# A state-space layer with a routed expert layer: the state-space part in a new pinned order, with other layouts for U and Y

## The chip, the cores and the metric

The kernel runs on one core of a Trainium2 chip. The metric is device time in microseconds (us) of one execution. The engines are called as the profile calls them: PE (matrix products; PEld is its weight load), DVE (vector), ACT (scalar, activation functions), POOL (GpSimd), and SP, whose queue issues most DMAs.

## The reference

Input x has 2 sequences of 2048 tokens with 128 channels. What is computed, cut to its core:

```python
def attn(x):                                   # on layernorm(x), as B=2 sequences
    u = swapaxes(x @ in_W.T + in_b, 1, 2)      # (B, D, L)
    dtA = (-exp(log_A_real) + 1j * A_imag) * exp(log_dt)[:, None]
    K = exp(dtA[:, :, None] * arange(L))       # 128 channels x 32 modes x L
    k = 2 * einsum('hn,hnl->hl', C * (exp(dtA) - 1) / A, K).real
    y = irfft(rfft(u, 2 * L) * rfft(k, 2 * L))[..., :L] + u * D_skip[:, None]
    a, g = split(glu_W @ gelu(y) + glu_b, 2)
    return swapaxes(a * sigmoid(g), 1, 2) @ out_W.T + out_b + x
def ffn(x):
    gates = softmax(x @ router_w)              # 14 routed experts, top 2, renormalised
    return sum over the top 2 of gate * expert(x) + shared_0(x) + shared_1(x)
x = x + attn(layernorm(x));  x = x + ffn(layernorm(x))   # expert: silu(rmsnorm(x) @ W1) @ W2
```

## The kernel before

**Tiles.** The 4096 tokens are 32 chunks of 128 (`NT` = 32, 16 per sequence). The long convolution is done chunk by chunk: inside a chunk by a 128 x 128 Toeplitz matrix per channel, between chunks by the 32 complex modes of each channel. Modes lie on partitions: 128 partitions are 4 channels x 32 modes, and `q` (`NQ` = 32) counts the groups of 4 channels, in four groups of 8 called group 0 to 3.

**State-space part, lines 173 to 537.** Token means (L189), turned copies of X through PE into XT, which is the memory of Y (L197, L198), and squares (L200) are on ACT. The mode arithmetic on DVE (L146 to L276, with two Sin on ACT, L237 and L238) ends in Z, the powers 1, 2, 4 ... 128 of each mode's factor. `double` (L292 to L301) builds PW, all powers 0 to 127, by seven doublings of four DVE operations each; the first five go over all q, the last two (m = 32, 64) over one group at a time. For each group follow

- `taps`: products of PW with BC on PE (L314, L319), four ACT copies into kk (L327), and a DMA of kk to memory (L329),
- `toeplitz`: DMAs that read the Toeplitz matrices back, 1 MB for each of 8 channel groups `toep[g]` (L344); numbers 5 and 6 go into the memory of Y, 0 to 4 and 7 share five buffers,
- `turned`: transposes of PW on PE (L353) and ACT copies into VT (L354).

Then `scales` (L362 to L369: reciprocal square roots on DVE, a product with `flip` on PE that turns them round), and `project` (L375 on PE, L380 on DVE), which make U, laid out chunk by chunk: `U[:, c, :]` is a chunk's 128 channels. Channel `h` of all chunks is therefore `U[:, :, h]`, 32 elements 512 B apart. L401 normalises X on ACT. W and E (L404 to L422, DVE) are the modes' powers over whole chunks. `chunk_sums` (L441, PE) reads VT and `U[:, :, h]`; `scan` (L465 to L486, DVE, once for each half of q) makes the states ST; `inside` (L509, PE) multiplies `U[:, :, h]` by the Toeplitz matrices, and L527 adds the states' part to the same PSUM tiles ("corrections"). Four of the eight channel groups are one half. After each half four Gelu (L533, ACT) write YC, and one DVE transpose of 32 x 32 blocks writes Y (L537), through a view with the token outermost.

**Gating and routing, lines 623 to 830.** Eight blocks of four chunks pass through `products` (pg, pa from Y on PE), `gate` (tanh `th` and `av` on ACT), `gated` (DVE), `project` (po), `add`, `scales`, `rows`, `logits`, `choose`, `count` and `scatter`; the last writes each token's row twice by indirect DMAs from POOL (L817, 64 in all). The shared experts run in between. All of these operations carry line 623, a helper. Their order is written out at the end of the function.

**Experts and end.** The loop over 45 tiles of routed rows (L889, L899, L908), then the sums per token.

**What sets the order.** A planner orders each engine's instructions and places the waits, except for those that pass through `tc.keep_in_program_order`: these keep the order of the program text on their engine. Before, V, S and T are wrapped so (class `Ordered`, L616) only from the gating part on; in the state-space part the planner is free, and it mixes, for instance, W's first operations into `scales`. The experts' loop is free again.

Of the kernel before, what the change touches and what calls it, by code (L numbers as in the profile page):

```python
# [18 lines left out]
P = 128  # L19
# [35 lines left out]
def swapped(ap):  # L55

    dims = [list(d) for d in ap.ap]
    step = dims[1][0]
    return bass.AP(ap.tensor, ap.offset + step, [dims[0], [-step, 2]] + dims[2:])


@with_exitstack
def s4d_glu_moe_kernel(
# [108 lines left out]
    Y = tokp.tile([P, NT, P], F32, name="Y")  # L172

    with ExitStack() as ssm:
        big = ssm.enter_context(tc.tile_pool(name="big", bufs=1))
        rot = ssm.enter_context(tc.tile_pool(name="rot", bufs=2))
        pss = ssm.enter_context(tc.tile_pool(name="pss", bufs=4, space=PSUM))


# [6 lines left out]
        XT = Y  # L186
        for b in range(B):
            for k in range(b * NCH, (b + 1) * NCH):
                S.activation(junk, X[:, k, :], AF.Copy, accum_out=nm[:, k:k + 1])  # L189
            G.tensor_scalar(  # L190
                nm[:, b * NCH:(b + 1) * NCH], nm[:, b * NCH:(b + 1) * NCH], -1.0 / P, None,
                ALU.mult,
            )
        for g in range(NB):
            pt = pss.tile([P, TB, P], F32, name=f"pt_{g}", tag="ps")
            for k in range(TB):
                T.matmul(pt[:, k, :], lhsT=X[:, g * TB + k, :], rhs=flip, start=True, stop=True)  # L197
            S.copy(XT[:, g * TB:(g + 1) * TB, :], pt)  # L198
        for k in range(NT):
            S.activation(  # L200
                junk, X[:, k, :], AF.Square, bias=nm[:, k:k + 1], accum_out=sq[:, k:k + 1]
            )

        cent = big.tile([P, P], F32, name="cent")
        G.tensor_scalar(cent, ident, 1.0 / P, None, ALU.subtract)
        pc = pss.tile([P, P], F32, name="pc", tag="ps")
        T.matmul(pc, lhsT=cent, rhs=inw, start=True, stop=True)
        inwc = big.tile([P, P], F32, name="inwc")
        S.copy(inwc, pc)
# [34 lines left out]


        R7 = big.tile([P, NQ], F32, name="R7")
        CS = big.tile([P, 2, NQ], F32, name="CS")
        S.copy(R7, mag[:, 7 * NQ:])
        S.copy(CS[:, 0], s2[:, 7 * NQ:])
        S.copy(CS[:, 1], s1[:, 7 * NQ:])  # L250

# [27 lines left out]
        tpp = ssm.enter_context(tc.tile_pool(name="toep", bufs=5))  # L279
# [8 lines left out]
        for c, x in ((0, 0), (1, 2)):  # L288
            V.tensor_tensor(
                BC[:, c], bc(CE[:, x], 2, 8), mask.rearrange("p g i a r -> p (g i a) r"), ALU.mult  # L290
            )

# [14 lines left out]
        def taps(g):  # L307
# [16 lines left out]
            kk = rot.tile([P, 2 * P], F32, name=f"kk_{g}", tag="kk", bufs=4)  # L324
            G.memset(kk, 0.0)
# [6 lines left out]
        def toeplitz(g):  # L332

            if g in (5, 6):
                tg = Y[:, 16 * (g - 5):16 * (g - 4), :]
            else:
                tg = tpp.tile([P, 4 * GQ, P], F32, name=f"toep_{g}", tag="toep")
# [18 lines left out]
        U = big.tile([P, NT, P], F32, name="U")  # L356
        rsr = big.tile([P, NT], F32, name="rsr")

        def scales():

            tc.keep_in_program_order(
                V.tensor_scalar(sq, sq, 1.0 / P, LN_EPS, ALU.mult, ALU.add)  # L362
            )
# [3 lines left out]
            V.tensor_copy(rsr, pf)  # L367
            V.tensor_tensor(nb, nm, rs, ALU.mult)
            V.tensor_scalar(rs1, rs, 1.0, None, ALU.add)  # L369

        def project(g):
            pu = pss.tile([P, TB, P], F32, name=f"pu_{g}", tag="ps")
            for k in range(TB):
                c = g * TB + k
                T.matmul(  # L375
                    pu[:, k, :], lhsT=XT[:, c, :], rhs=inwc, start=True, stop=True
                )
            for k in range(TB):
                c = g * TB + k
                V.scalar_tensor_tensor(  # L380
                    U[:, c, :], pu[:, k, :], rsr[:, c:c + 1], inb, ALU.mult, ALU.add
                )

        for m in (1, 2, 4, 8, 16):
            double(slice(0, NQ), m)
        for g in range(4):
# [3 lines left out]
            for n in (2 * g, 2 * g + 1):  # L390
                if n < 5:
                    toeplitz(n)
            turned(g)
        scales()
        for b in range(NB):
            project(b)
        toeplitz(5)
        toeplitz(6)

        for k in range(NT):  # L400
# [3 lines left out]


        W = big.tile([P, 2, NQ, NCH], F32, name="W")
        E = big.tile([P, 2, NQ, NCH], F32, name="E")
        V.tensor_copy(W[:, :, :, 0], CS)
        for m in (1, 2, 4, 8):
            t1 = rot.tile([P, 2, NQ, m], F32, name="t1w", tag="t1", bufs=1)  # L410
            t2 = rot.tile([P, 2, NQ, m], F32, name="t2w", tag="t2", bufs=1)
            low, top = W[:, :, :, 0:m], W[:, :, :, m - 1]
            V.tensor_tensor(t1, low, bc(bc(top[:, 0], 1, 2), 3, m), ALU.mult)
            V.tensor_tensor(t2, low, bc(bc(top[:, 1], 1, 2), 3, m), ALU.mult)
            V.tensor_tensor(W[:, 0, :, m:2 * m], t1[:, 0], t2[:, 1], ALU.subtract)
            V.tensor_tensor(W[:, 1, :, m:2 * m], t1[:, 1], t2[:, 0], ALU.add)
        t1 = rot.tile([P, 2, NQ, NCH], F32, name="t1e", tag="t1", bufs=1)
        t2 = rot.tile([P, 2, NQ, NCH], F32, name="t2e", tag="t2", bufs=1)
        V.tensor_tensor(t1, bc(CE[:, 0:2], 3, NCH), bc(W[:, 0], 1, 2), ALU.mult)
        V.tensor_tensor(t2, bc(CE[:, 0:2], 3, NCH), bc(W[:, 1], 1, 2), ALU.mult)  # L420
        V.tensor_tensor(E[:, 0], t1[:, 0], t2[:, 1], ALU.add)
        V.tensor_tensor(E[:, 1], t1[:, 1], t2[:, 0], ALU.subtract)  # L422

        RA = big.tile([P, NQ * B, NCH], F32, name="RA")
        G.memset(RA[:, :, 0:1], 0.0)
        S.copy(
            RA[:, :, 1:].rearrange("p (q b) i -> p q b i", b=B), bc(bc(R7, 2, B), 3, NCH - 1)
        )
        ST = big.tile([P, 2, NQ, NT], F32, name="ST")
        G.memset(ST.rearrange("p c q (b i) -> p (c q b) i", b=B)[:, :, 0:1], 0.0)  # L430

        HQ = NQ // 2
        with tc.tile_pool(name="psS", bufs=2, space=PSUM) as psS:

            def chunk_sums(x):

                sp = psS.tile([P, 2, HQ, NT], F32, name=f"SP_{x}", tag="sp")
                for q in range(x * HQ, (x + 1) * HQ):
                    for c in range(2):
                        for j in range(4):  # L440
                            T.matmul(  # L441
                                sp[j * NM:(j + 1) * NM, c, q - x * HQ, :],
                                lhsT=VT[:, c, q, j * NM:(j + 1) * NM], rhs=U[:, :, 4 * q + j],
                                start=True, stop=True,
                            )
                return sp

            def scan(x, sp):


                qs = slice(x * HQ, (x + 1) * HQ)
                er, ei = bc(E[:, 0, qs], 2, B), bc(E[:, 1, qs], 2, B)
                wr, wi = (bc(W[:, c, qs, :NCH - 1], 2, B) for c in range(2))

                def four(what, n):
                    ts = [
                        rot.tile([P, 2, HQ, B, n], F32, name=f"{what}{i}_{x}", tag=f"t{i}", bufs=1)
                        for i in (1, 2)
                    ]
                    return [t[:, i] for t in ts for i in range(2)]  # L460

                s0, s1 = (sp[:, c].rearrange("p q (b i) -> p q b i", b=B) for c in range(2))
                D = rot.tile([P, 2, HQ, B, NCH], F32, name=f"D_{x}", tag="D", bufs=1)
                a, b, c, d = four("d", NCH)
                V.tensor_tensor(a, s0, er, ALU.mult)  # L465
                V.tensor_tensor(b, s1, ei, ALU.mult)
                V.tensor_tensor(D[:, 0], a, b, ALU.subtract)
                V.tensor_tensor(c, s0, ei, ALU.mult)
                V.tensor_tensor(d, s1, er, ALU.mult)
                V.tensor_tensor(D[:, 1], c, d, ALU.add)  # L470
                QS = rot.tile([P, 2, HQ, B, NCH], F32, name=f"QS_{x}", tag="QS", bufs=1)
                for i in range(2):
                    V.tensor_tensor_scan(
                        QS[:, i].rearrange("p q b i -> p (q b i)"),
                        RA[:, B * qs.start:B * qs.stop, :].rearrange("p q i -> p (q i)"),
                        D[:, i].rearrange("p q b i -> p (q b i)"), 0.0, ALU.mult, ALU.add,
                    )
                a, b, c, d = four("e", NCH - 1)
                q0, q1 = QS[:, 0, :, :, :NCH - 1], QS[:, 1, :, :, :NCH - 1]
                st = ST[:, :, qs].rearrange("p c q (b i) -> p c q b i", b=B)[:, :, :, :, 1:]  # L480
                V.tensor_tensor(a, q0, wr, ALU.mult)
# [670 lines left out]
```

## Time and profile before

| | |
|---|---|
| median of 3 runs | 402.42 us (401.95 to 404.42) |
| the profiled execution | 408.15 us |
| its span, first to last instruction | 406.1 us |
| mean granted PE clock | 0.848 |
| busy PE, DVE, ACT, POOL | 292.5, 223.2, 169.4, 161.3 us |
| transpose into Y ends | 123.1 us |
| first scatter, last scatter issued | 148.2, 252.0 us |

The profiled execution is 5.7 us longer than the median, so times read from its rows are set against its own span, and only differences are carried over to the median. A row of the timeline has the start, the duration, the engine, the line, the operation, its output and inputs, and their shapes; in square brackets stands how long the engine had been idle, and what ended that. A row of the groups has the busy time and the mean of one in ns, then the idle time before. Neighbouring rows of one engine can overlap a little, so the time that an instruction really takes on its engine is the distance from start to start.

### The profile page before, as it was taken

The page shows a single profiled execution, that of the slowest core. Times are in us where ns is not written, and L with a number is a line of the kernel's source. Part 1 is how long each engine was busy: PE and PEld are TensorE (multiplying, and loading weights), DVE is VectorE, ACT ScalarE, POOL GpSimd, SP SyncE. Part 2 cuts the span into 40 slices and gives each one's busy share as a digit, 9 for nine tenths or more (in the row PEclk, how much of TensorE's full clock was granted, in tenths as well). Part 3 has the DMA queues.
Part 4 walks back from the last instruction along what each step waited for, and adds up shares of the span by engine and source line. Part 5 has one row for each costly group of instructions (what it writes and reads, how often), then busy time and mean ns, then how long its engine had stood idle before and what let it go on. Part 6 is the DMA issues. An engine that isn't in the chain of part 4 may idle for free. (4 is left out here: it accounts for less than half of the span.)

```text
span 406.1 us, 7923 instructions
## 1 busy us (share of the span) xinstructions
PE 292.5 (72%) x2800; PEld 236.8 (58%) x2800; DVE 223.2 (55%) x654; ACT 169.4 (42%) x388; POOL 161.3 (40%) x243
## 2 busy tenths in 40 slices
PE   2702777788907647999999956599988879799500
PEld 2701567787903433768676644499977768797400
DVE  5699989899753662774958330133332333231074
ACT  3999869400431526485857502122222212132100
POOL 4300000000002034027677777057777777777500
PEclk9965889899965866696968989599999999899955
DMA  8100379913006911001111112665555555630098
GB/s 232 24 1 2 85 209 248 241 46 64 5 0 216 347 50 39 2 7 52 49 52 53 54 53 78 225 231 192 197 195 198 195 196 184 213 111 17 4 370 246
DMA packets 58089, 50.63 MB, mean 125 GB/s; under 512 B 6669, under 2 KB 50203, under 8 KB 58050
## 3 DMA queue, kind: packets, MB, share of 16 engines
q1 hardware_dynamic: 51010, 40.60, 32.8%
q0 software_dynamic: 4928, 8.48, 6.1%
q10 hardware_dynamic: 2112, 1.05, 0.9%
q8 instruction: 22, 0.36, 0.4%
q14 instruction: 17, 0.14, 0.1%
HBM read 25.36 MB, written 14.64 MB: 98 GB/s over the span
## 5 line engine op out<-in xcount | busy, mean ns | idle before, releaser
L908 POOL DMA_INDIRECT res<-yo,xg x90 | 88.6, 984 | 41.3 <-issue 19.8
L817 POOL DMA_INDIRECT xs_rows<-pl,si x64 | 62.0, 969 | 65.4 <-issue 39.1
L891 ACT ACTIVATE hs<-ph 128x512 f32<-128x512 f32 x45 | 26.9, 597 | 90.8 <-PE ph L889 90.8
L904 DVE TENSOR_TENSOR yo<-pz,xg 128x256 f32<-128x256 f32 x45 | 19.1, 424 | 60.9 <-PE pz L899 49.7
L899 PEld LDWEIGHTS pz<-wg,hs 128*128 128x128 f32 x360 | 48.0, 195 | 2.4
L889 PE MATMUL ph<-xgt,wg 128*128 128x256 f32 x180 | 49.4, 401 | 0.0
L899 PE MATMUL pz<-wg,hs 128*128 128x128 f32 x360 | 48.0, 278 | 0.0
L582 POOL MEMSET blank<- 128x260 f32 x1 | 0.3, 315 | 96.1 <-DVE Y L537 96.1
L889 PEld LDWEIGHTS ph<-xgt,wg 128*128 128x128 f32 x180 | 32.8, 203 | 3.0
L881 PE MATMUL xgt<-ident,xg 128*128 128x128 f32 x90 | 19.6, 302 | 18.3 <-DMA xg<-xs_rows 18.1
L883 DVE COPY xgt<-xgt 128x256 f32<-128x256 f32 x45 | 18.8, 418 | 22.4 <-PE xgt L881 22.3
L623 PE MATMUL ph<-XRT,WB 128*128 128x512 f32 x48 | 27.0, 712 | 0.3 <-ACT hsh L623 0.3
L623 ACT ACTIVATE hsh<-ph 128x512 f32<-128x512 f32 x24 | 14.1, 597 | 28.6 <-PE ph L623 28.6
L623 PEld LDWEIGHTS pz<-WB,hsh 128*128 128x128 f32 x192 | 22.9, 192 | 3.8 <-issue 3.6
L881 PEld LDWEIGHTS xgt<-ident,xg 128*128 128x128 f32 x90 | 10.9, 149 | 22.8 <-DMA xg<-xs_rows 21.4
L623 PE MATMUL pz<-WB,hsh 128*128 128x128 f32 x192 | 23.1, 275 | 0.0
L314 PE MATMUL kps<-PW,BC 128*8 128x128 f32 x128 | 5.6, 307 | 21.9 <-ACT junk L200 18.4
L623 PE MATMUL po<-outwh,y 128*128 128x128 f32 x64 | 15.4, 427 | 7.7 <-DVE y L623 7.7
L623 PEld LDWEIGHTS po<-outwh,y 128*128 128x128 f32 x64 | 14.0, 326 | 10.2 <-issue 6.8
L623 PE MATMUL pg<-Y,gluw 128*128 128x512 f32 x16 | 12.0, 844 | 10.8 <-DVE Y L537 10.8
L623 PEld LDWEIGHTS ph<-XRT,WB 128*128 128x128 f32 x48 | 10.7, 236 | 12.4 <-issue 10.7
L441 PE MATMUL SP<-U,VT 128*32 128x32 f32 x512 | 13.9, 301 | 5.5 <-issue 3.0
(236 smaller groups left out, 569.3 us busy)
## 6 DMA issues: line engine op xcount, KB each, us to landing
wg<-WB SPq DMA_DIRECT2D x45, 256.0 KB, 2.7
toep<-kp SPq DMA_DIRECT2D x24, 256.0 KB, 6.3
xg<-xs_rows SPq DMA_DIRECT2D x45, 130.0 KB, 2.3
WB<-res SPq DMA_DIRECT2D x7, 512.0 KB, 4.0
Y<-kp SPq DMA_DIRECT2D x8, 256.0 KB, 3.9
xs_rows<-blank SPq DMA_DIRECT2D x1, 1820.0 KB
WB<-in_w_dram SPq DMA_DIRECT2D x2, 896.0 KB
WB<-in_w_dram SPq DMA_DIRECT2D x4, 448.0 KB, 7.2
```

The lines of the kernel that those rows point to most:

```text
L314: T.matmul(kps[a * NM:a * NM + 8, :], lhsT=BC[:, c, q, :], rhs=PW[:, c, q, 0:P], start=(i == 0 and c == 0), stop=False, skip_group_check=True,
L441: T.matmul(sp[j * NM:(j + 1) * NM, c, q - x * HQ, :], lhsT=VT[:, c, q, j * NM:(j + 1) * NM], rhs=U[:, :, 4 * q + j], start=True, stop=True,)
L582: G.memset(blank, 0.0)
L623: return tc.keep_in_program_order(getattr(self.engine, name)(*args, **kwargs))
L817: G.indirect_dma_start(out=xs_part[2 * (k0 + k) + a], out_offset=bass.IndirectOffsetOnAxis(ap=si[:, a, k:k + 1], axis=0), in_=pl[:, a, k, ...
L881: T.transpose(pt[:, s * P:(s + 1) * P], xg[:, s, :P], ident)
L883: V.tensor_copy(xt, pt[:, :2 * P])
L889: T.matmul(ph[:, f], lhsT=wg[:, f * P:(f + 1) * P], rhs=xt, start=True, stop=True)
L891: S.activation(hs, ph, AF.Silu)
L899: T.matmul(pz[:, s * P:(s + 1) * P], lhsT=hs[:, f, s * P:(s + 1) * P], rhs=wg[:, HID + f * P:HID + (f + 1) * P], start=(f == 0), stop=(f = ...
L904: V.tensor_tensor(yo, pz[:, :2 * P].rearrange("p (s d) -> p s d", s=2), bc(xg[:, :, P], 2, P), ALU.mult)
L908: G.indirect_dma_start(out=res_part[2 * t + s], out_offset=bass.IndirectOffsetOnAxis(ap=xg[:, s, P + 1:P + 2].bitcast(I32), axis=0), in_=y ...
```

## The change

- **Order.** `Ordered` now wraps S, T and G from the beginning of the state-space part, and V from the end of the mode arithmetic; G stays wrapped to the end of the kernel, V, S and T are free in the experts' loop as before.
- **Statistics.** Squares are taken from `px`, a product of XT with the centring matrix `cent` (new PE work), instead of from X with the mean as bias. They and six of the eight turned copies now stand behind the two Sin. The token sums stand behind the squares: 12 ahead of the taps of group 0, 20 behind the turns of group 0.
- **W and E** are computed on POOL, with the same formulas and in tiles of their own.
- **U** is laid out `[P, 128 channels, 32 chunks]` and made behind group 0, not behind group 3. `rs` needs no turning for it (XT and px are both turned); the turned one is needed only for rs1, which ACT now writes.
- **Between groups**: chunk sums 0 and 1 and `inside` 0 and 1 are spread between the groups; chunk sums and `inside` 2 and 3 follow group 3. All Toeplitz reads are issued in the groups' order, with four shared buffers for five. RA's copy and X's normalisation follow group 3.
- **PSUM**: four buffers `pse` during the statistics, afterwards two each of `pss` and `psY`; two double ones, `psS`, throughout.
- **End**: for the second half each Gelu is split into four ranges of tokens, and each quarter is transposed as it is ready. Y is laid out `[P, 128 tokens, 32 chunks]`.
- **Gating**: the products read `Y[:, :, 4j:4j+4]`; `th` and `av` are written back into chunk order.

The diff, cut to its core:

```diff
-    Y = tokp.tile([P, NT, P], F32, name="Y")
+    Y = tokp.tile([P, P, NT], F32, name="Y")
...
+        S, T, G = Ordered(tc, S), Ordered(tc, T), Ordered(tc, G)
...
+        def squares(g):
+            px = pss.tile([P, TB, P], F32, name=f"px_{g}", tag="ps")
+            for k in range(TB):
+                T.matmul(
+                    px[:, k, :], lhsT=XT[:, g * TB + k, :], rhs=cent, start=True, stop=True
+                )
+            for k in range(TB):
+                c = g * TB + k
+                S.activation(junk, px[:, k, :], AF.Square, accum_out=sq[:, c:c + 1])
+        def sums(k0, k1):
+            for k in range(k0, k1):
+                S.activation(junk, X[:, k, :], AF.Copy, accum_out=nm[:, k:k + 1])
+        turned_tokens(0)
+        turned_tokens(1)
...
         V.tensor_tensor(Z[:, 1].rearrange("p k q -> p (k q)"), mag, s1, ALU.mult)
+        for g in range(NB):
+            squares(g)
+            if g + 2 < NB:
+                turned_tokens(g + 2)
...
+        W = big.tile([P, 2, NQ, NCH], F32, name="W")
+        G.tensor_copy(W[:, 0, :, 0], s2[:, 7 * NQ:])
+        G.tensor_copy(W[:, 1, :, 0], s1[:, 7 * NQ:])
...
+        pss = ssm.enter_context(tc.tile_pool(name="pss", bufs=2, space=PSUM))
+        psY = ssm.enter_context(tc.tile_pool(name="psY", bufs=2, space=PSUM))
+        V = Ordered(tc, V)
+        tpp = ssm.enter_context(tc.tile_pool(name="toep", bufs=4))
...
+        for m in (1, 2, 4, 8):
+            t1 = big.tile([P, 2, NQ, m], F32, name="t1w", tag="t1w")
+            t2 = big.tile([P, 2, NQ, m], F32, name="t2w", tag="t2w")
+            low, top = W[:, :, :, 0:m], W[:, :, :, m - 1]
+            G.tensor_tensor(t1, low, bc(bc(top[:, 0], 1, 2), 3, m), ALU.mult)
+            G.tensor_tensor(t2, low, bc(bc(top[:, 1], 1, 2), 3, m), ALU.mult)
+            G.tensor_tensor(W[:, 0, :, m:2 * m], t1[:, 0], t2[:, 1], ALU.subtract)
+            G.tensor_tensor(W[:, 1, :, m:2 * m], t1[:, 1], t2[:, 0], ALU.add)
+        t1 = big.tile([P, 2, NQ, NCH], F32, name="t1e", tag="t1w")
+        t2 = big.tile([P, 2, NQ, NCH], F32, name="t2e", tag="t2w")
+        G.tensor_tensor(t1, bc(CE[:, 0:2], 3, NCH), bc(W[:, 0], 1, 2), ALU.mult)
+        G.tensor_tensor(t2, bc(CE[:, 0:2], 3, NCH), bc(W[:, 1], 1, 2), ALU.mult)
+        G.tensor_tensor(E[:, 0], t1[:, 0], t2[:, 1], ALU.add)
+        G.tensor_tensor(E[:, 1], t1[:, 1], t2[:, 0], ALU.subtract)
...
-        U = big.tile([P, NT, P], F32, name="U")
+        U = big.tile([P, P, NT], F32, name="U")
...
+        def projected(x):
+            pu = psp.tile([P, 2 * TB, P], F32, name=f"pu_{x}", tag="sp")
+            for k in range(2 * TB):
                 T.matmul(
+                    pu[:, k, :], lhsT=XT[:, 2 * TB * x + k, :], rhs=inwc, start=True, stop=True
                 )
+            return pu
+        def scaled_u(x, pu, rs):
+            for k in range(2 * TB):
+                c = 2 * TB * x + k
                 V.scalar_tensor_tensor(
-                    U[:, c, :], pu[:, k, :], rsr[:, c:c + 1], inb, ALU.mult, ALU.add
+                    U[:, :, c], pu[:, k, :], rs[:, c:c + 1], inb, ALU.mult, ALU.add
                 )
...
+        sums(0, 12)
+        pus = [projected(x) for x in range(2)]
         for m in (1, 2, 4, 8, 16):
             double(slice(0, NQ), m)
         for g in range(4):
             for m in (32, 64):
                 double(slice(8 * g, 8 * g + 8), m)
             taps(g)
             for n in (2 * g, 2 * g + 1):
-                if n < 5:
-                    toeplitz(n)
+                toeplitz(n)
             turned(g)
+            if g == 0:
+                rs = scales()
+                for x in range(4):
+                    scaled_u(x, pus[x], rs)
+                    if x < 2:
+                        pus.append(projected(x + 2))
+                sums(12, NT)
+            if g < 2:
+                chunk_sums(g)
+            if g == 0:
+                inside(0)
+                inside(1)
+        for g in (2, 3):
+            chunk_sums(g)
+            inside(g)
+        S.copy(
+            RA[:, :, 1:].rearrange("p (q b) i -> p q b i", b=B), bc(bc(R7, 2, B), 3, NCH - 1)
+        )
...
+            parts = 1 if half[0] == 0 else 4
+            w = P // parts
+            for x in range(parts):
+                for g in half:
+                    S.activation(
+                        YC[:, x * w:(x + 1) * w, GQ * g:GQ * g + GQ].rearrange("p t q -> p q t"),
+                        ysum[g][:, :, x * w:(x + 1) * w], AF.Gelu,
+                    )
+                if parts > 1:
+                    V.transpose(
+                        Y[:, x * w:(x + 1) * w], YC[:, x * w:(x + 1) * w],
+                    )
...
-            yt = Y[:, j * TB:(j + 1) * TB, :].rearrange("p k t -> p (k t)")
+            yt = Y[:, :, j * TB:(j + 1) * TB]
...
+            by_token = lambda t: t.rearrange("p (k t) -> p t k", k=TB)
+            S.activation(by_token(th), pg, AF.Tanh, bias=glubh, scale=0.5)
...
+            S.activation(by_token(av), pa, AF.Identity, bias=glub[:, 0:1])
```

`chunk_sums(g)` in the new code takes one group of q; before, `chunk_sums(x)` took one half of q.

## The prediction

> **What bounds the kernel now.** I read the page's 40 slices first (10.15 us each).
>
> ```profile
> PE   2702777788907647999999956599988879799500
> DVE  5699989899753662774958330133332333231074
> ACT  3999869400431526485857502122222212132100
> POOL 4300000000002034027677777057777777777500
> ```
>
> Up to slice 10 DVE is the full engine and POOL is empty; that is the state-space part, and it ends with the transpose into Y at 123.1 us. From slice 17 on POOL is full. The timeline of the first part, the lines that I lean on:
>
> ```profile
> 21.49 0.43 DVE L242 TENSOR_TENSOR Z<-mag,s 128x256 f32<-128x256 f32 x1
> ...
> 37.34 0.68 DVE L301 TENSOR_TENSOR PW<-t,t 128x512 f32<-128x512 f32 x1
> ...
> 61.71 8.35 DVE L380 SCALAR_TENSOR_TENSOR U<-pu,rsr,inb 128x128 f32<-128x128 f32 x32
> ...
> 79.69 1.87 DVE L465 TENSOR_TENSOR d<-SP,E 128x512 f32<-128x512 f32 x1 [0.95 <-PE SP L441]
> ...
> 93.31 0.68 DVE L465 TENSOR_TENSOR d<-SP,E 128x512 f32<-128x512 f32 x1
> ...
> 105.19 7.19 PE L527 MATMUL yps<-PW,ST 32*32 32x128 f32 x256
> ...
> 112.41 3.59 ACT L533 ACTIVATE YC<-yps 128x512 f32<-128x512 f32 x4 [5.94 <-PE yps L527]
> ...
> 116.02 7.08 DVE L537 STREAM_TRANSPOSE Y<-YC 128x4096 f32<-128x4096 f32 x1 [6.52 <-ACT YC L533]
> ```
>
> DVE is in one chain: Z ready 21.9, powers of group 0 ready 38.0, of group 3 at 55.5, U at 70.1, W and E at 78.7, scan 0 until 93.3, scan 1 until 104.3; then PE until 112.4, Gelu, transpose. The same instruction L465 takes 1.87 us in scan 0 and 0.68 in scan 1. While it is long, PE runs L441 or L509, which read U with a step of 512 B; L527 and L375, which read contiguously, leave DVE alone. The first group of the last half shows it again (L483 1.86 instead of 0.65 while L509 runs). Scan 1 took 11.0 us, of which its last three ops lost about 2 in this way; unhindered a scan is 9.0. So the strided U costs some 4.6 us in scan 0, 4.5 in W and E (8.7 us against 4.2), 2 in scan 1.
>
> The second part:
>
> ```profile
> 179.96 0.96 POOL L817 DMA_INDIRECT xs_rows<-pl,si  x1 [21.77 <-ACT av L623]
> 181.22 1.10 POOL L817 DMA_INDIRECT xs_rows<-pl,si  x1 [0.30 <-ACT pl L623]
> ...
> 251.96 0.96 POOL L817 DMA_INDIRECT xs_rows<-pl,si  x1 [0.30 <-issue]
> ```
>
> From 180 us POOL issues scatters one each 1.26 us with one gap of 2.4, until the expert loop. So what ends earlier before 123 moves everything behind it by as much, and what is later in the gating between 123 and 180 too; behind 180 little counts.
>
> **The parts, and the sum without any new contention.** Sums are on the profiled clock (408.15 us, span 406.1); the difference is then taken from the median 402.42.
>
> Mode chain: the Sin of rr (ready at 13.4) waited on ACT behind token sums, turned copies and a table load; DVE idled 2.9 us at L239. Now only two turned copies stand ahead: table 1.28, two Sin 0.84, then L239, L240, L242 at 1.2: Z at 17.0, 4.9 us earlier. Powers to group 0 took 38.0-21.9 = 16.1 us: 33.1. The memset of PW's column 0 is now pinned on POOL behind W's first column, which needs s2 (16.7): about 17.6. The CE arithmetic, 3 us of DVE that is among the 16.1, covers that; if it were not free to go first, 0.6 us come out.
>
> ACT: the 32 token sums (0.435 us start to start) and squares (0.527) are still there; squares now read PSUM, I take 0.45 (0.435 to 0.527). With 6 turned copies at 0.5 and 0.8 of small copies: 15.6+14.4+3+0.8 = 34, with 12 sums 39. The new px products, 64 passes like L375's (7.6 us for 64), run on PE beside the squares, at 0.95 us a block against ACT's 1.8, so they cost nothing while ACT is the slower one. Then the kk copies of group 0, its VT copies, the other 20 sums (8.7 us, until 51). Taps 0 on PE wait behind the last px and projections anyway (37 to 38). These sums now stand ahead of group 1's kk copies; they are hidden if U takes DVE until then, otherwise up to 8.7 us come out.
>
> U behind group 0: scales 3.5 us (55.5 to 59.0), then 32 L380 at 0.26, now written with a step of 128 B. No row has that on DVE; lower end 0.26, upper 0.35 (the strided transpose's 1.73 ns an element against 1.11 of a plain 1024-element op, times 128). I take 0.34: 10.9 us. The third block of U waits for its projection, which PE does behind group 0's turns: 1.6 us. Groups 1 to 3: 17.5 us (38.0 to 55.5). Group 3 done: 33.1+3.5+10.9+1.6+17.5 = 66.6. VT of group 3 followed its powers by 5.1 us (55.5 to 60.6); with two PSUM buffers for four I take 5.6: 72.2.
>
> PE from there, in its written order: chunk sums 2 and 3 with gaps 3.8 each (512 L441 took 16.8, a quarter 4.2, of which instruction gaps 0.8), inside 2 and 3 at 0.96; half 0's corrections 8.45 (92.87 to 101.32), four insides 3.87, corrections 7.2: 29.0. DVE's two scans at 9.0 from 66.6, with a wait of 2 to 3 us at the scan itself for RA's copy, which now stands on ACT behind VT 3 (until 73), end near 90, before half 1's corrections are due (93); all that is queued behind the waiting scan on DVE is scan 1, which has 3 us to spare, and X + outb (5.3 us), which only the transposes follow. `nb` and `rs1`, moved behind the doublings and to ACT, are small and wait for nothing late. SP: with four Toeplitz buffers for five, reads of 4 to 7 are queued behind inside(0), inside(1) and the XT reads (all over by 55), and each kp write behind the reads before it, yet their 6.5 us a group are done by 87, ahead of use at 89 or later. X's 32 normalisations on ACT (15.4 us) end about when half 0's Gelu is due.
>
> End: Gelu in 16 pieces. 512 elements took 0.90 each in L533; 128 cost between 0.22 (a 128-element ACT op, start to start) and 0.43; I take 0.35, 5.6 us. The last quarter's transpose 1.2 us (1.14, a 1024-element DVE op, to 1.77, a quarter of L537). With 0.1 for starts, 6.9 instead of 10.75. Y ready at 72.2+29.0+6.9 = 108.1 instead of 123.1: **15.0 us earlier**.
>
> Gating: th and av are written with a step of 512 B. Near rows:
>
> ```profile
> L533 ACT ACTIVATE YC<-yps 128x512 f32<-128x512 f32 x8 | 7.5, 1094 | 6.0 <-PE yps L527 5.9
> L623 ACT ACTIVATE th<-pg,glubh 128x512 f32<-128x512 f32 x8 | 5.5, 686 | 15.9 <-PE pg L623 15.9
> ```
>
> L533 (128 B step) is 0.4 us longer; bounds 0 and 0.4 for each, and I take 0.4 for four that lie on the way to POOL (first av, the th that the fourth pa waits for at 159.7, two in ACT's row at 175.9 to 179.1): **+1.6 us**. The products read Y four tokens at a time, 16 B in each 128 B. By the nearest row, L441's strided reads, DVE beside 22.6 us of pg and pa would slow 1.5-fold, some 3 us before 180. [...] I take 0.
>
> **W and E on POOL.** 20 operations of 5952 output elements leave DVE and run beside its doublings. Rows:
>
> ```profile
> 26.93 0.25 POOL L190 TENSOR_SCALAR nm<-nm 128x16 f32<-128x16 f32 x1 [9.32 <-ACT junk L189]
> 26.95 0.72 DVE L299 TENSOR_TENSOR t<-PW,Z 128x512 f32<-128x512 f32 x1
> ...
> 32.83 0.68 DVE L299 TENSOR_TENSOR t<-PW,Z 128x512 f32<-128x512 f32 x1
> ```
>
> The one L299 that met a POOL op is 0.04 us longer than the four later ones of its size: 2.5 ns for each of 16 elements. POOL itself goes from 258 ns (16 elements) to 544 (128): 2.55 ns an element. [...] Held time: 5952 x 2.55 = 15.2 us by the row[...]; I take 13.9, all before 50 us and so on group 0's chain. The projection wait of 1.6 disappears in it: group 3 at 66.6+13.9-1.6 = 78.9, Y ready at **120.4**, 2.7 us earlier than before. By the trace's idle POOL alone the sum would be 402.4-15.0+1.6 = 389.0; by the rule 402.4-2.7+1.6 = 401.3. With the small row on the rule's side, I take the rule.
>
> **Rivals.**
> POOL is hidden (no exclusion, or DVE wins each time and POOL works beside U, whose L380 has one SBUF tensor): 389.0. For it: E is due only at 67 us, and POOL's 0.96 us scatters never change beside DVE. Against it: the 0.04 us.
> Half of the held time comes out: 13.9/2 less on the chain, 395.
> Slower: POOL holds each instruction whole. Its fixed 0.22 us, and up to 0.25 more for patterns in four dimensions (dsk's copy, 32 elements, 0.505 us), times 20: 4.4 to 9.4 us on top, 405.7 to 410.7, say 408. It decides from 15.0 us held on (no gain left); 1% slower from 19.
> The change not doing its work: the strided reads' 4.6 and 2 us and the transpose's 3.8 do go, but PE's tail (29 us behind VT 3) is as long as DVE's was, which is why the rule's case ends near zero.
>
> **How the numbers follow.** Rule's case 0.42, own range 397.5 to 405 (U 0.26 to 0.35 is -2.6 to +0.3, RA and PSUM waits and clock of the gating stage +-3). Hidden 0.22, half 0.16, slower 0.20. A measurement tells about 1% (398.4 to 406.4). Faster: 0.10+0.22+0.14 = 0.46; within: 0.30+0.02+0.05 = 0.37; slower: 0.02+0.15 = 0.17. 388 to 408 leaves out about a third of the hidden case and half of the slower one, under 0.2.
>
> **What would show it.** DVE's 1024-element doublings over 1.22 us between 17 and 50, group 0 at 47 (33 if hidden); POOL's 20 operations 20 us in sum or more; d rows back to 0.68 beside the chunk sums; U rows at 0.34; 5.6+1.2 us behind the last correction; th at 1.1. Wrong would be: the doublings at 1.22 beside POOL, PE waiting for Toeplitz reads, or group 1's kk copies late behind the 20 sums.

## The result and the profile after

| | before | after |
|---|---|---|
| median, same chip, in turn | 403.43 us (401.24 to 405.94, 15 runs) | 400.07 us (397.40 to 403.05, 15 runs) |
| ratio, 95% interval | | 0.9915 (0.9887 to 0.9944) |
| span of the profiled execution | 406.1 us | 398.3 us |
| mean granted PE clock | 0.848 | 0.866 |
| Y ready | 123.1 us | 119.8 us |
| first, last scatter issued | 148.2, 252.0 us | 144.3, 245.6 us |

The change gained 3.4 us of the medians, 0.85%; 401.3 had been predicted, from 388 to 408. Executions in a slower state, which some runs below have, count in their medians, not in their ratios. Of the 7.8 us between the two spans Y accounts for 3.3; the profiled execution of before lay 4.7 us above its median (408.15 against 403.43), that of after on its median.

All pinned instructions now carry line 70, the wrapper, so the rows are known by their tiles. The page's slices (9.96 us each):

```profile
DVE  5999979979343761867667340133323233321074
POOL 4792000000002043037777775067777777777500
```

POOL has work up to 32 us. In the eleventh slice DVE falls to 3 (7 before): there the end belongs to PE. The timeline of DVE and POOL while W and E run, and one row from behind that time:

```profile
17.33 0.46 POOL L70 TENSOR_TENSOR t1w<-W 128x128 f32<-128x128 f32 x1
...
25.46 3.86 DVE L70 TENSOR_TENSOR PW<-t,t 128x32 f32<-128x32 f32 x2
...
27.32 1.93 POOL L70 TENSOR_TENSOR t2e<-CE,W 128x1024 f32<-128x1024 f32 x1
...
29.36 2.66 DVE L70 TENSOR_TENSOR t<-PW,Z 128x128 f32<-128x128 f32 x2
...
35.90 2.36 DVE L70 TENSOR_TENSOR t<-PW,Z 128x1024 f32<-128x1024 f32 x2
```

Two DVE instructions of 32 elements took 3.86 us together (0.32 where POOL is still, in run 1), two of 128 took 2.66 (0.50). From 32 us on nothing is long any more: two of 1024 take 2.36, start to start 1.2 each. POOL lost much less: its 1024-element t1e took 1.93 us both here and where DVE read only one operand from SBUF (run 1, at 46.70), and its 16 operations for W took 9.8 us from first to last, against 8.9 in run 8.

The later rows, which answer to those shown of before:

```profile
47.89 4.34 DVE L70 SCALAR_TENSOR_TENSOR U<-pu,rq_y,inb 128x128 f32<-128x128 f32 x16
54.47 4.33 DVE L70 SCALAR_TENSOR_TENSOR U<-pu,rq_y,inb 128x128 f32<-128x128 f32 x16 [2.24 <-PE pu L70]
...
88.66 1.29 DVE L70 TENSOR_TENSOR d<-SP,E 128x512 f32<-128x512 f32 x2 [0.46 <-PE SP L70]
...
106.88 7.19 PE L70 MATMUL yps<-PW,ST 32*32 32x128 f32 x256
114.12 3.67 ACT L70 ACTIVATE YC<-yps 128x128 f32<-128x128 f32 x16 [8.59 <-PE yps L70]
115.18 4.62 DVE L70 STREAM_TRANSPOSE Y<-YC 128x1024 f32<-128x1024 f32 x4 [11.88 <-ACT YC L70]
```

U's strided writes cost next to nothing (0.27 us each, 0.26 before); the d rows take 0.66 each from start to start while PE's insides read U (until 90.3); the end is 5.75 us, in which the four transposes follow each other. Between 81 and 114 us PE has four gaps for which the profile names no releaser:

```profile
87.75 0.80 PE L70 MATMUL SP<-U,VT 128*32 128x32 f32 x43 [3.79 <-issue]
...
93.55 3.70 PE L70 MATMUL yps<-PW,ST 32*32 32x128 f32 x128 [1.49 <-issue]
98.10 2.38 PE L70 MATMUL yps<-PW,ST 32*32 32x128 f32 x78 [0.85 <-issue]
...
104.57 1.40 PE L70 MATMUL yps<-Y,U 128*32 128x128 f32 x43 [2.44 <-issue]
```

They sum to 8.6 us; the prediction had at most 0.8 in each of two chunk sums. Before, PE's gaps from 70 to 113 us came to 3.4. Run 9, the same program, has 6.0, so a part of the 8.6 belongs to this one execution. The granted clock, too, fell in this stretch: 0.79 from 88 to 94 us, 1.00 from 94 to 114.

### The profile page after: what moved, and what is told of

It is laid out like the page before. It is cut to its first block, busy times and chain, and to the rows that moved or that the text cites. A ratio compares the mean times of both kernels' runs of the same rounds, so it can differ in the third digit from the quotient of the medians.

```text
span 398.3 us, 8082 instructions
## 1 busy us (share of the span) xinstructions
PE 291.3 (73%) x2864; PEld 230.5 (58%) x2864; DVE 215.8 (54%) x635; ACT 170.0 (43%) x399; POOL 176.3 (44%) x263
## 5 line engine op out<-in xcount | busy, mean ns | idle before, releaser
L946 PEld LDWEIGHTS pz<-wg,hs 128*128 128x128 f32 x360 | 47.0, 192 | 2.2
L936 PE MATMUL ph<-xgt,wg 128*128 128x256 f32 x180 | 48.0, 392 | 0.0
L946 PE MATMUL pz<-wg,hs 128*128 128x128 f32 x360 | 47.1, 275 | 0.0
L928 PE MATMUL xgt<-ident,xg 128*128 128x128 f32 x90 | 19.6, 301 | 19.2 <-DMA xg<-xs_rows 19.0
L70 DVE TENSOR_TENSOR t<-PW,Z 128x512 f32<-128x512 f32 (+4 forms) x26 | 23.1, 930 | 0.4
L70 ACT ACT_TABLE_LOAD x13 | 16.7, 1283 | 13.3 <-PE yps L70 6.1
L70 PE MATMUL po<-outwh,y 128*128 128x128 f32 x64 | 13.1, 378 | 7.5 <-DVE y L70 7.5
L70 PEld LDWEIGHTS po<-outwh,y 128*128 128x128 f32 x64 | 11.8, 279 | 10.7 <-DVE y L70 7.0
```

Source lines behind the costliest of these rows:

```text
L70: return self.tc.keep_in_program_order(getattr(self.engine, name)(*args, **kwargs))
L928: T.transpose(pt[:, s * P:(s + 1) * P], xg[:, s, :P], ident)
L936: T.matmul(ph[:, f], lhsT=wg[:, f * P:(f + 1) * P], rhs=xt, start=True, stop=True)
L946: T.matmul(pz[:, s * P:(s + 1) * P], lhsT=hs[:, f, s * P:(s + 1) * P], rhs=wg[:, HID + f * P:HID + (f + 1) * P], start=(f == 0), stop=(f = ...
```

## Experiments

Ratios are to the kernel before, run in turn on the same chip, with 95% intervals.

**1. The same work of POOL, a little later.** W and E stay on POOL, but a flag holds them until the scales are done, so that they begin beside the scaling of U, whose instructions read one operand from PSUM.

```diff
+        def we(G):
+
...
                 rs = scales()
+                flag = big.tile([P, 2], F32, name="flag")
+                V.tensor_copy(flag[:, 0:1], rs[:, 0:1])
+                G.tensor_copy(flag[:, 1:2], flag[:, 0:1])
+                we(G)
```

> The 20 operations of W and E stay on POOL but start only behind the scales, beside the making of U, whose DVE instruction has one SBUF tensor. Exclusion theory: the first doublings run free, group 0's powers end near 33.5 us instead of 45.4; U's instructions stay at 0.27; what is left of POOL's 16 us (some 3 to 6 us) falls on group 1's doublings; the chain gains 5 to 9 us, time 391 to 395. Rival, the doublings are slow because the pinned order lost the mixing of independent work (no exclusion): group 0 stays near 45 and the time within 2 us of 400.

Measured: 395.42 us, ratio 0.978 (0.9721 to 0.984), at the upper end of the range. Group 0 was done at 34.9 instead of 45.4, 17.5 us behind Z; the U rows kept 0.27 us beside POOL. E's part ran over into group 1, and there DVE was held again; its timeline:

```profile
43.78 4.36 DVE L70 SCALAR_TENSOR_TENSOR U<-pu,rq_y,inb 128x128 f32<-128x128 f32 x16 [1.98 <-PE pu L70]
47.99 3.53 DVE L70 TENSOR_TENSOR t<-PW,Z 128x512 f32<-128x512 f32 x2
51.55 2.78 DVE L70 TENSOR_TENSOR PW<-t,t 128x256 f32<-128x256 f32 x2
54.36 2.36 DVE L70 TENSOR_TENSOR t<-PW,Z 128x1024 f32<-128x1024 f32 x2
```

3.53 and 2.78 stand for 1.29 and 0.76 us unhindered. So POOL's work cost nothing beside U, and what ran over cost 4.3 us beside the doublings; there POOL was slowed too, its t2e to 2.38 us. Y was ready at 114.2. So DVE's own chain from Z to the end of group 0 is 17.5 us, and what POOL held up in the changed kernel is 28.2 - 17.5 = 10.7 us.

**2. W and E on DVE** at the same place.

```diff
-            G.tensor_tensor(t1, low, bc(bc(top[:, 0], 1, 2), 3, m), ALU.mult)
+            V.tensor_tensor(t1, low, bc(bc(top[:, 0], 1, 2), 3, m), ALU.mult)
```

(and so for all 20.)

> The same 20 operations at the same place of the text, but on DVE. Exclusion theory: DVE pays their own 8 to 9 us (by the rows of before) instead of the 12.2 us of being shut out, group 0 near 42, time 396 to 398. Rival (POOL takes nothing from DVE, the order is slow in itself): 8 us come on top, time 406 to 409.

Measured: 401.88 us, ratio 0.9898 (0.9846 to 0.9951): between the two ranges, and not to be told from the changed kernel's by time. The trace tells more: the 20 take DVE 8.8 us (20.35 to 29.15), group 0 is done at 43.8, Y at 117.0. On POOL the same work delayed DVE by 10.7 us, more than doing it.

**3. POOL only writes.** Each of the 20 becomes a memset of the same output; what W and E hold is left out.

```diff
-            G.tensor_tensor(t1, low, bc(bc(top[:, 0], 1, 2), 3, m), ALU.mult)
+            G.memset(t1, 0.5)
```

> Leaves out the arithmetic of W and E: each of POOL's 20 operations is a memset of the same output, so POOL is busy at the same place but reads nothing. If it is POOL's reading that shuts DVE out: doublings at 1.22 us, group 0 near 33.5, time 388 to 393. If any POOL access to SBUF does (writes too): group 0 40 or later, time 396 or more. If POOL has nothing to do with it: group 0 near 45, time near 400.

Measured: 394.43 us, ratio 0.9723 (0.9681 to 0.9765), group 0 done at 40.2: between the first case and the second. DVE's timeline beside the memsets (16.7 to 22.8):

```profile
17.75 0.42 DVE L265 TENSOR_TENSOR Z<-mag,s 128x256 f32<-128x256 f32 x1
18.09 4.79 DVE L290 TENSOR_SCALAR wz<-Z 128x32 f32<-128x32 f32 x1
```

L265, a product of two SBUF tensors, took 0.42 us beside memsets, as long as in run 1, where POOL was still. But L290, one input of 32 elements, took 4.79 us instead of 0.17 (run 1), until the last memset had ended. The longest group of memsets here took 0.98 us, so it was held over several of them. From Z to the end of group 0 passed 22.0 us, 4.5 of them held, all on L290 and on the copy L291 beside it. The memsets were over before the first doubling, so no doubling was tried against writes.

**4. U as before**, 512 B between a channel's chunks, all else as changed.

```diff
-        U = big.tile([P, P, NT], F32, name="U")
+        U = big.tile([P, NT, P], F32, name="U")
...
-                    U[:, :, c], pu[:, k, :], rs[:, c:c + 1], inb, ALU.mult, ALU.add
+                    U[:, c, :], pu[:, k, :], rs[:, c:c + 1], inb, ALU.mult, ALU.add
...
-                            lhsT=VT[:, c, q, j * NM:(j + 1) * NM], rhs=U[:, 4 * q + j, :],
+                            lhsT=VT[:, c, q, j * NM:(j + 1) * NM], rhs=U[:, :, 4 * q + j],
```

> U laid out as before, chunk by chunk; chunk sums and inside read it with a step of 512 B, all else as in the changed kernel. Theory (strided reading slows PE itself and DVE beside it): 128 chunk-sum passes take 3.4 us again instead of 1.45 (8 us in all, half of it in PE's tail), doublings and d instructions beside them 1.2 to 3 times longer, time 4 to 9 us above the changed kernel, 404 to 409. Rival, the slow DVE of before came from the DMA traffic of that time: DVE rows stay at 0.68 and 1.22, time within 2 us of 400.

Measured: 406.77 us, ratio 1.0029 (0.9995 to 1.0063): without the new U the change gains nothing. DMAs ran beside the doublings of the changed kernel too (share 0.81 to 0.91 from 70 to 76 us) and did not slow them (two of 1024 elements 2.36 us), so the rival falls. The timeline shows PE's chunk sums and its neighbours:

```profile
57.90 3.60 DVE L70 TENSOR_TENSOR t<-PW,Z 128x512 f32<-128x512 f32 x2
...
69.17 4.29 ACT L70 COPY VT<-vps 128x512 f32<-128x512 f32 x4
71.12 4.19 PE L70 MATMUL SP<-U,VT 128*32 128x32 f32 x128
71.74 3.82 DVE L70 TENSOR_TENSOR PW<-t,t 128x512 f32<-128x512 f32 x2
```

The 128 passes take 3.2 to 4.2 us instead of 1.45, and while they run DVE's two instructions of 512 elements take 3.6 to 3.8 instead of 1.3, and ACT's four copies 4.29 instead of 2.64. (PE was slower ahead of the chunk sums at 58 us also without U: the 32 products `kps` took 2.07 us at 44.9, but 1.35 to 1.41 at 66.3, 75.1 and 81.0, around the rows from 69 us on.) Y was ready at 124.0.

**5. One transpose of half 1 in place of four.**

```diff
-            parts = 1 if half[0] == 0 else 4
+            parts = 1
```

(the one transpose follows half 1's Gelu.)

> The last 512 columns of Y come from one Gelu and one contiguous transpose instead of four of each. Theory (the quarters overlap ACT and VectorE): ACT takes about 3.7 us, then VectorE about 4.6 us, together 8.3 us where the changed kernel has 5.75 between the end of the last correction and the end of Y, so Y is 2.6 us later and the time 0.6% above the changed kernel (ratio to before 0.998). Rival (one large instruction of each has less fixed cost, and the quarters give nothing): 5.75 to 6.5 us and a ratio of 0.990 to 0.993.

Measured, in a round in which the kernel before took 458.89 us instead of 404.73 (why is not known; the part up to Y takes as long as elsewhere, what follows is slower): 458.41 us, ratio 0.9981 (0.9946 to 1.0017). ACT 3.58, then DVE 4.45; Y is ready 8.1 us behind the last correction instead of 5.75. The quarters are worth 2.4 us in the trace.

**6. Y laid out as before**, so that the quarters are strided again and the gating is contiguous.

```diff
-    Y = tokp.tile([P, P, NT], F32, name="Y")
+    Y = tokp.tile([P, NT, P], F32, name="Y")
```

> Y is kept with the channel-block index outermost as before, and the quarter transposes write it with a step; the gating reads and writes contiguously again. The strided quarters should take 1.77 us each as in the kernel before, so that the part after the last correction grows from 5.75 to about 8.2 us (Y 2.5 us later). Theory of the prediction (the token-outermost layout costs 1.6 us in the gating): the gating's activations go back from 1.13 to 0.69 us and the stretch from Y to the second unit's scatter is 1.0 to 1.8 us shorter, so the whole is only 0.9 us slower than the changed kernel (ratio 0.994). Rival (the layout costs the gating nothing, because those activations are not on its path): the stretch keeps its length, the whole is 2.5 us slower (ratio 0.998).

Measured in the same round: ratio 1.0003 (0.9973 to 1.0034). The quarters took 1.77 us each, and the end is 8.2 us. th and av went back from 1.13 to 0.69 us each, yet from Y to the first scatter passed 25.1 us against 25.5 in run 5, and to the second unit's first 56.9 against 56.1. The times of runs 5 and 6 can't be told apart; the ratio leaves out the theory's 0.994. The profiled execution of run 6 took 468.06 us, 10.7 above its median; before the change, with the same old layout, the two stretches were 25.1 and 56.9, after it 24.5 and 55.7. So no profile shows a gain in the gating from the old layout. The granted clock up to the second unit's scatter differs, though: 0.71 before the change, 0.77 after it. Up to the first scatter it is 0.70 and 0.71.

**7. Half of the Toeplitz reads left out**: blocks 4 to 7 are not read, 0 to 3 stand in for them.

```diff
         def toeplitz(g):
 
+            if g >= 4:
+                toep[g] = toep[g - 4]
+                return
```

> The Toeplitz blocks 4 to 7 are not read: blocks 0 to 3 are used in their place, so half of the Toeplitz part is left out of the result. TensorE's work keeps its number of instructions. Theory (the gaps of 8.6 us called issue in TensorE's tail come from the traffic of these reads): the gaps vanish or fall below 2 us, the tail behind the last turned powers is 25 to 27 us instead of 32.9, and the ratio to before is 0.972 to 0.978. Rival (the gaps belong to the sequencer and to the code it loads, whatever the DMA queues do): the gaps stay at 7 to 9 us and the ratio at 0.989 to 0.993.

Measured in the same round: ratio 0.9842 (0.977 to 0.9914), between the two ranges, which had been reckoned from 403 us. The trace decides; PE's timeline:

```profile
84.39 0.60 PE L70 MATMUL SP<-U,VT 128*32 128x32 f32 x45 [1.87 <-issue]
...
87.15 6.97 PE L70 MATMUL yps<-PW,ST 32*32 32x128 f32 x248 [0.85 <-DVE ST L70]
94.06 3.70 PE L70 MATMUL yps<-toep,U 128*32 128x128 f32 x128
97.69 7.26 PE L70 MATMUL yps<-PW,ST 32*32 32x128 f32 x256
```

Of 8.6 us of gaps 1.87 are left, and PE's tail behind VT 3 is 24.9 us instead of 32.9. The granted clock is 1.00 from 70 to 105 us. The gap that is left comes with the DMA engines empty (share 0.00 from 82 to 85 us), so it isn't the reads'.

**8. What follows from 1 to 4.** W alone stays on POOL, behind the scales, and is over before group 1; E's four go to DVE behind group 3, where it waits for PE; RA is copied while ACT is idle in group 0; chunk sums 2 come ahead of group 3's taps.

```diff
                 rs = scales()
+                flag = big.tile([P, 2], F32, name="flag")
+                V.tensor_copy(flag[:, 0:1], rs[:, 0:1])
+                G.tensor_copy(flag[:, 1:2], flag[:, 0:1])
+                powers_w()
...
-            if g < 2:
+            if g < 3:
                 chunk_sums(g)
...
+        ends_e()
```

> From the changed kernel: only the powers W stay on GpSimd, held back until the scales are done, so that they run beside the projection's scaling, which takes one operand from PSUM; E's four instructions go to VectorE behind the last group of powers, where it waits for TensorE; ScalarE's fill of RA is made while ScalarE is idle in group 0; the chunk sums of group 2 come ahead of group 3's taps. Theory (what matters is which VectorE instructions GpSimd's reads of SBUF run beside): group 0 ends at 35, W ends before group 1's first doubling or within 1.5 us of it, so group 3 is done at 65 to 67 instead of 69.65 when W and E both ran beside the scaling; E adds nothing; RA and the chunk sums give 2 to 4 us; together 4 to 7 us below that kernel, ratio to before 0.962 to 0.970. Rival (the end is set by TensorE's gaps and reads of the Toeplitz blocks, so an earlier group 3 gives nothing back): Y within 1 us of that kernel's 114.2, ratio 0.976 to 0.980.

Measured in the round of runs 5 to 7: 447.21 us, ratio 0.9813 (0.9754 to 0.9872). The ratio missed both ranges; the places came out, but Y gained 3.5 us on run 1, not 4 to 7: W ends at 46.7, group 3 at 65.1 with no doubling held, Y at 110.8.

**9 and 10. The changed kernel and run 8 again, together on another chip** (no new edit).

> The changed kernel unaltered, so that the two runs beside it have it as a second yardstick on one chip. Both theories: ratio to before 0.989 to 0.995, Y ready at 119 to 121 us.

> The kernel with W beside the scaling, E on VectorE, RA early and group 2's chunk sums early, once more, beside the changed kernel. Theory (the 9 us by which Y came earlier in it are kept to the end): 9 us below the changed kernel, ratio to before 0.967 to 0.973. Rival (what follows Y takes part of it back, as the 64 scatters and the experts wait for other things): 3 to 6 us below it, ratio 0.976 to 0.984.

Measured: the changed kernel 399.29 us, ratio 0.9857 (0.9809 to 0.9904), 0.3 points below its range, with an interval that meets the first one; run 8's kernel 391.23 us, ratio 0.9626 (0.9575 to 0.9677), 0.4 points below its range. Between the two lie 8.1 us by the medians and some 9 by the ratios, so about all of the 9 us by which Y is earlier in these two (118.7 against 109.8) reach the end.

**11. The last kp write ahead of block 5's reads** on SP's queue, in run 8's kernel.

```diff
-            for n in (2 * g, 2 * g + 1):
+            for n in ((0, 1), (2, 3), (4,), (5, 6, 7))[g]:
                 toeplitz(n)
```

> The kernel above, and the last write of kernel taps is issued on SP's queue behind the reads of block 4, ahead of those of block 5, so that its 5.5 us of landing run beside block 5's reads. Theory (TensorE's gaps and waits come from the Toeplitz reads, which now end 4 us earlier, at about 88): the gap of 2.7 and the waits of 1.1 us in the insides of blocks 4 to 7 vanish, Y is 2 to 4 us earlier than in the kernel above, ratio 0.5 to 1.0% lower. Rival (a gap belongs to every stretch of so much code while any reads run, and moves with them): the gaps keep their sum of 7 to 8 us and Y is within 1 us of the kernel above.

Measured: 388.23 us, ratio 0.9588 (0.9542 to 0.9634), 3.0 us below run 10 by the medians and 0.4% by the ratios, with intervals that overlap: a gain not clear of the noise. In the trace the last read is issued at 87.4 (92.0 in run 8), PE's gaps sum to 3.3 us (7.8 in run 8, 5.8 in run 10), no pass waits for a Toeplitz block any more, and Y is ready at 107.4 (110.8 and 109.8). The gap in the insides of blocks 4 to 7, expected to vanish, shrank only to 1.62. Of the 2.4 us between the Y of runs 10 and 11, 1.5 are the last corrections (8.86 and 7.35 us), which the edit does not touch. This is the fastest version found.

## Why the prediction was right

The mechanism of the likeliest case held: DVE's doublings were shut out beside POOL, and PE's tail took the rest of the gain. Predicted was a gain of 1.1 us; it was 3.4, and 1.6 of the difference are the gating term, which did not show. Its terms, by their places:

| step | predicted | measured |
|---|---|---|
| Z | 17.0 | 17.1 |
| Z to the end of group 0 | 30.0 = 16.1 + 13.9 held | 28.2 = 17.5 + 10.7 held |
| scales and U | 14.4 | 13.3 |
| groups 1 to 3 | 17.5 | 17.4 |
| VT 3 behind them | 5.6 | 5.15 |
| PE behind VT 3 | 29.0 | 32.9 |
| end | 6.9 | 5.75 |
| Y ready | 120.4 | 119.8 |
| gating | +1.6 | -0.6 to the first scatter, -1.2 to the second unit's |

That Y came within 0.6 us of its place is partly luck: terms that were too long by 4.6 us in sum and terms that were too short by 4.0 cancelled.

**The exclusion**, the prediction's rule, was the author's estimate, with one row that was 0.04 us longer to show for it. It was the point on which the cases parted, and runs 1 to 3 settle it: DVE was held for 10.7 us beside POOL's 20. Run 1 changes only when POOL runs, and Y comes 5.6 us sooner. The rival "hidden" falls by the same run (of the scatters that were counted for it, 61 of 64 took 0.95 or 0.96 us before the change, three 1.10 to 1.25), and the held time lies between "half" (7.0) and the 13.9 taken: of the 14.7 us between Z and the end of POOL's 20, DVE still used 4.0. The slower rival falls too: it needed more than 15.0 us held. The sign that was named, doublings of 1024 elements over 1.22 us, did not come: POOL was done at 32 us, before DVE reached them, and the small instructions were held instead.

POOL's 20 took 16.3 us from first to last, where 15.2 had been reckoned from a row and 13.9 taken, the author's estimate; of the 16.3, 1.6 lay ahead of Z and 4.0 DVE still used. DVE's own 16.1 us was 1.4 too low: before, CE's small dependent instructions alternated with the first doublings, at 0.10 to 0.21 us from start to start; one behind the other they are 0.11 to 0.26 apart (run 8), and the doublings stand behind them. From Z's copy wz to the third doubling passed 3.1 us before, 4.7 in run 8.

**PE's tail** is the step that failed, twice and in opposite senses. The chunk sums were taken from strided reads (3.8 each); contiguous ones take 1.45, which is 4.7 us less for two. The gaps were taken as a quarter of those in the chunk sums of before, 0.8, and as nothing in the insides and corrections. PE's rows of before show what the mean hid:

```profile
79.11 3.46 PE L441 MATMUL SP<-U,VT 128*32 128x32 f32 x128 [2.47 <-issue]
83.11 3.94 PE L441 MATMUL SP<-U,VT 128*32 128x32 f32 x138 [0.54 <-issue]
```

The long gap fell beside reads (DMA share 0.95 from 70 to 80 us), the short one, like the 0.35 at 97.04, where they were over (0.15 from 80 to 90, 0.02 from 96 to 102). And the prediction had the reads done by 87. SP's queue after the change:

```profile
75.80 0.60 SPq L385 DMA_DIRECT2D kp<-kk  x1
80.84 2.02 SPq L400 DMA_DIRECT2D toep<-kp  x4
...
87.72 0.81 SPq L385 DMA_DIRECT2D kp<-kk  x1
93.42 2.01 SPq L400 DMA_DIRECT2D Y<-kp  x4
95.53 5.16 SPq L400 DMA_DIRECT2D toep<-kp  x4
```

Each kp write stood behind the reads ahead of it, and the next read was issued 5.0 and 5.7 us after the write. So the reads of blocks 4 to 7 (80.8 to 100.7 us) lay over PE's densest code. Run 4 shows the step's price and run 7 the reads'. Without the gaps the tail would have been 24.3; run 7 has 24.9, of which 2.7 are its own gap and a wait for ST. The other 2.1 us between them are passes that were slower in the changed kernel, where the granted clock fell (30 passes of an inside at 88.4 took 1.90 us, 32 of one in run 7 took 1.08); what lowered the clock is not shown.

The gaps stand at fixed places of the code, 127 or 128 matmuls with as many weight loads apart. The page has two rows for instruction queues, of which one is:

```profile
q8 instruction: 23, 0.38, 0.4%
```

(packets, MB, share). PE's 2864 matmuls and as many weight loads are 5728 instructions, 249 for each packet; before they were 5600, with 22 packets in the row, 255 for each. So the gaps could be waits for PE's instructions themselves: the author's estimate, from the spacing and these counts; no trace shows such a wait, nor whose queue the row is. Beside the reads four gaps took 0.85 to 3.8 us each, and only the first, just as they began, 0.28. That the reads cause most of it is shown by run 7. The 1.87 us left with the queues empty stays open; PE had gone through the 128 before it in some 1.8 us, where 128 corrections take 3.7.

**U and the end** were mis-sized by an estimate where no row was near: 0.27 instead of 0.34 a row, and 0.23 instead of 0.35 us for a Gelu of 128. The transposes then set the end. The wait for the projection, which I let vanish, stayed at 2.2 us. **Gating**: th and av cost the predicted 0.4 us more each, yet with them the stretch to the first scatter is no longer (24.5 us against 25.1), at granted clocks of 0.71 and 0.70. Up to the second unit's scatter the clocks differ (0.77 against 0.71), so whether they were off the path there, or PE's higher clock made up for them, stays open. The 0 for the products' reads of Y was the author's estimate; DVE's 66 instructions from Y to the first scatter were busy for 13.55 us before and 13.56 after.

The gain is small because what was won was paid out again in two waits that the change itself made: 10.7 us on DVE beside POOL, and 5.2 more than before in PE's gaps (8.6 - 3.4). Without both, and if nothing else had come to bind, Y would have come 19.2 us earlier (3.3 + 10.7 + 5.2, an estimate); in run 11 it comes 15.7 us earlier (123.1 - 107.4).

## What to carry to other kernels

Moving work to an idle engine was free here only beside the right instructions: DVE's U rows, with one operand in PSUM, kept their 0.27 us beside POOL, while four of its doublings, with two operands in SBUF, took 6.31 us instead of 2.05 (run 1). So list what runs at the same time and where its operands lie, and try the work beside instructions that read PSUM. When an order is rewritten, ask for each stretch of dense code which transfers now run over it, since its gaps were measured beside others (PE's here came to 8.6 us with all the reads and to 1.87 with half of them), and do not spread a sum of gaps as a mean. A stride was paid for by the neighbours as well as by the reader: PE's 128 passes took 4.19 us instead of 1.45, and two DVE instructions of 512 elements beside them 3.82 instead of 1.29 (run 4).

## What the hardware showed beyond that

- POOL won against DVE again and again: it kept its 1.93 us for 1024 elements while two 32-element rows of DVE rose from 0.32 to 3.86 us; even memsets held a one-input row for 4.79 us (run 3). Beside longer rows of DVE it lost a little: 2.38 us beside two of 512 (run 1).
- PE's reads with a step of 512 B slow ACT as well as DVE: four copies 4.29 instead of 2.64 us (run 4).
- A step in what is written can cost nothing or much: DVE's 128-element rows with 128 B between elements took 0.27 us where the contiguous ones took 0.26, while ACT's 512-element th rows with 512 B took 1.13 instead of 0.69, and DVE's quarter transposes with 512 B 1.77 instead of 1.15. Whether the engine or the step decides is not shown.
